# Layer 0 of a four-layer graph network: single-head rows, pair sums in their own buffers, later counts, more kept tiles and a moved quarter of weights

## The chip, the cores and the metric

The kernel runs on one core of a Trainium2 chip. The metric is the device time in microseconds of one execution of the whole program. Three runs of the kernel before took 3268.78, 3267.47 and 3268.74 us; their median is 3268.74.

A core has five engines that run side by side, each in its own order of instructions: TensorE (PE, matrix products; PEld is its loading of weights), VectorE (DVE), ScalarE (ACT), GpSimd (POOL) and SyncE (SP). SP, POOL and ACT also issue transfers between the chip's memory (HBM, "dram" in the code) and the on-chip memory of 128 partitions (SBUF). Matrix products are accumulated in another small memory, PSUM.

## What is computed

Four graph layers follow each other, each with a residual and a layer norm. Only layer 0 is changed. Its input is x (2708 x 512) and a 0/1 matrix adj (2708 x 2708). Both patterns of layer 0 are the same adj.

```python
Xh = X.reshape(n, H, D).transpose(1, 0, 2)          # H = 4 heads, D = 128
Xw = jnp.einsum('hnd,hde->hne', Xh, W)
f1 = jnp.einsum('hnd,hd->hn', Xw, V[:, 0, :, 0])
f2 = jnp.einsum('hnd,hd->hn', Xw, V[:, 1, :, 0])
sig = jax.nn.sigmoid(f1[:, :, None] + f2[:, None, :])
att = softmax(where(adj != 0, adj * sig, -inf))      # 0 outside the mask
Xa = jnp.einsum('hij,hjd->hid', att, Xw)             # first use of att
Xn = batchnorm(Xa)                                   # over the 2708 rows
emb = batchnorm(elu(Xn @ W1.T + b1) + Xn)
Y = jnp.einsum('hij,hjd->hid', att, emb)             # second use of the same att
Y = elu(jnp.einsum('hnd,hed->hne', Y, W))
out = batchnorm(elu(Y @ W2.T + b2) + Y)
```

## The kernel before, in words

**Tiles.** The attention is made transposed: the rows of a tile are 128 values of j, the columns are values of i. There are 22 tiles of j (BLOCKS; the last has only 20 rows) and the 2708 columns are cut in two halves of 1354 (HSPAN). The four heads are taken in two pairs, p = 0 and p = 1. A *block* is one half with one pair; a block has 22 *places*, one tile of j at each, in the order of ORDER (line 154): tiles 0 to 10, the short tile 21, then 11 to 20. A pass over the attention is four blocks: half 0 with pairs 0 and 1, then half 1 with pairs 0 and 1. In this text the first pass (values xw, the output Xa) has blocks 0 to 3, the second (values emb, the output Y) blocks 4 to 7. "5:1" is place 1 of block 5.

**One place** (`form`, line 360, and `attention_pass`, line 336). A row of the mask, a (128 x 1354, 677 KB), is loaded from HBM by SP. The mask is adj itself in blocks 0 and 2, where DVE turns it into 1 and -1e30 (line 389) and POOL writes it back as adj_d; later blocks load adj_d. ACT takes tanh of half of f1 + f2 for each of the two heads (line 400), where f1b holds f1 spread over the partitions, both heads of the pair in one tile, in one of two buffers, and f2 is a bias per partition. DVE multiplies tanh + 1 with the mask row (line 408), a product over both heads at once, 2708 columns. ACT takes exp of it (line 409). The tile t is then multiplied with the values by TensorE (line 478): two heads times three column parts of 452, each matmul in two passes. The six results stay in PSUM over all 22 places. In the second pass DVE also counts, once per tile and half, how many entries of the mask row are zero (`count`, line 342, one instruction on line 350); before, this stands ahead of the tile's tanhs and product, in the block of the pair that isn't read back. There are four t buffers, and four a buffers in the first pass, three in the second.

**Sums of the softmax.** In the first pass a product with ones (line 507, into psm) sums each tile over j. In blocks 0 and 2 every tile is summed. In blocks 1 and 3 the places from 4 to 19 (ALONE, LAST) are summed in pairs: DVE adds the odd tile into the even one (line 498), and TensorE sums the result. The pair's addition and sums are kept back (`waiting`) and put ahead of the matmuls of the next even place, the addition behind that place's product. Since the even tile is overwritten, the addition waits for TensorE to have read it. In the second pass the sums are already known; their inverses are loaded as rb.

**Kept tiles.** Some of the finished t tiles are written to HBM in the first pass by POOL (line 457, 1354 KB each), and read back in the second (line 460) in place of forming them anew. KEPT (line 160) lists their places for each pair: five and five, with place 11 common to both. A common tile is counted in the block of pair 0 from a mask row of its own (line 462).

**Ends of blocks.** A finished block's results leave PSUM before the next block's first matmuls can overwrite them: in the first pass by copies in `keep` (line 590), half of them on ACT, half on DVE; in the second by DVE's multiplication with rb and the batch norm's scale in `decode` (`take`, line 846, six per block).

**Between the passes.** Batch norm 1, the preparation of layer 3's weights, and the MLP with elu and batch norm 2. For layer 3 the product of its two weight matrices is wanted. `merged(c)` (line 696) makes a quarter of it with four matmuls. Two quarters are made here; the other two are made at the end of layer 0, after the last block's dec matmuls (line 985), copied by ACT (line 993) and written by POOL (line 994).

**What sets the order.** Each engine runs its instructions in one fixed order[...]. The program's text gives the work; a planner of the framework sets each engine's order when the kernel is built, by the costs it assumes and by when buffers come free. `tc.issue_after(x)` puts what is inside it behind instruction x. A tile with a tag shares its buffers with all tiles of that tag; a new one waits until the oldest is no longer read.

## Time and profile before

The times come from the three runs, the rest from one execution taken by the profiler.

| what | value |
|---|---|
| median of three runs | 3268.74 us (3267.47 to 3268.78) |
| the profiled execution, its own time | 3272.62 us |
| its span in the trace | 3270.8 us, 30357 instructions |
| PE busy | 3212.9 us, 98% |
| DVE busy | 1944.1 us, 59% |
| ACT busy | 1346.8 us, 41% |
| POOL busy | 132.9 us, 4% |
| transfers | 384.59 MB, mean 118 GB/s |
| DVE product, line 408, 2708 columns | 2976 ns on average, 156 times |
| ACT tanh, line 400, 1354 columns | 1413 ns, 312 times |
| ACT exp, line 409, 2708 columns | 2453 ns, 156 times |
| DVE pair addition, line 498, 2708 columns | 2974 ns |
| DVE count, line 350, 1354 columns | 1562 ns |
| mean granted clock of TensorE | 0.994 |

How to read it: a line of the groups gives source line, engine, operation, what it writes from what, the shape and the number of instructions; behind the first bar the busy time and the mean of one in ns; behind the second the time that the engine idled just before these instructions, and what ended that idling. A line of the chain gives the start and the length in us of a piece of the chain of waits that ended last. A line of the windows gives the busy time of each engine in a stretch, with its number of instructions, then the clock granted to TensorE (1.00 is full speed), the share of the DMA engines and GB/s.

Layer 0 takes about the first 1190 us of the span: block 0 begins at 44.5 us with its first matmul, the middle part lies from 556 to 670 us, and the second pass ends near 1121 us. Layers 1 to 3 follow.

### The profile page before, as it was taken

Reading aid. Unit: us, or ns where it says so; the run is one execution under the profiler, and the core shown is the slowest. Engines: PE = TensorE matmul, PEld = TensorE weight load, DVE = VectorE, ACT = ScalarE, POOL = GpSimd, SP = SyncE. Lnnn points to the kernel's source line nnn. Section 1 sums busy time; section 2 is a strip of 40 time slices with the busy share of each in tenths; the row PEclk is TensorE's granted clock in tenths of the full one; section 3 lists DMA queues with packets and bytes.
Section 4 is the critical chain, followed back from the end, with each engine's and each line's share of the span. In section 5 each row is a group of like instructions: output and inputs, shape, how many; then the busy total and the mean of one; then the engine's idle time right before and its main releaser. Section 6 shows DMA issues by size and latency. Waiting matters only on the chain.

```text
span 3270.8 us, 30357 instructions
## 1 busy us (share of the span) xinstructions
PE 3212.9 (98%) x10906; PEld 1717.4 (53%) x10906; DVE 1944.1 (59%) x3144; ACT 1346.8 (41%) x1512; POOL 132.9 (4%) x215
## 2 busy tenths in 40 slices
PE   8999999999999999999999999999999999999999
PEld 5444444444444446885555555544455555555554
DVE  7878977867687685445136666777353442543433
ACT  6888886567868652001133434443021020110211
POOL 1100100000000000000010000000000000000000
PEclk9999999999999999999999999999999999999999
DMA  7856854245545412550034444553211111111100
GB/s 278 314 187 223 298 200 147 88 152 194 169 163 177 169 53 80 144 133 15 1 118 136 118 124 137 151 160 111 72 47 32 45 35 37 41 34 45 35 24 20
DMA packets 173158, 384.59 MB, mean 118 GB/s; under 512 B 21034, under 2 KB 115190, under 8 KB 168334
## 3 DMA queue, kind: packets, MB, share of 16 engines
q1 hardware_dynamic: 157214, 309.74, 31.1%
q0 software_dynamic: 15792, 72.91, 5.9%
q8 instruction: 86, 1.41, 0.2%
q14 instruction: 66, 0.54, 0.1%
HBM read 308.79 MB, written 73.24 MB: 117 GB/s over the span
## 4 chain that ended last, share of the span: by engine, by line
PE 87%; DVE 6%; ACT 3%; DMA 2%; issue 1%; SPq 0%; DVEq 0%; ACTq 0%
PE po L1377 23%; PE po L478 18%; PE ps_s L1256 17%; PE ps_nb L1109 7%; PE ps_wide L1158 4%; PE psm L507 3%; DVE t L408 2%; PE ps_hid L129 2%; PE ps_sup L1554 2%; PE ps_o L1485 2%; PE ps_dec L880 2%; ACT t L400 2%; ACT t L409 1%; PE ps_mlp L755 1%; DMA a<-adj_d 1%
## 5 line engine op out<-in xcount | busy, mean ns | idle before, releaser
L408 DVE SCALAR_TENSOR_TENSOR t<-t,a 128x2708 f32<-128x2708 f32 (+1 forms) x156 | 462.4, 2976 | 135.2 <-ACT t L400 131.2
L400 ACT ACTIVATE t<-f1b,f2h 128x1354 f32<-128x1354 f32 (+1 forms) x312 | 427.2, 1413 | 63.5 <-PE psm L507 32.1
L409 ACT ACTIVATE t<-t 128x2708 f32<-128x2708 f32 (+1 forms) x156 | 382.2, 2453 | 95.0 <-DVE t L408 94.8
L478 PE MATMUL po<-t,xw 128*128 128x452 f32 (+3 forms) x1056 | 412.9, 553 | 7.7 <-ACT t L409 7.7
L478 PE MATMUL po<-t,emb 128*128 128x452 f32 (+3 forms) x1056 | 403.1, 550 | 12.5 <-ACT t L409 9.2
L1256 PE MATMUL ps_s<-sup,hT 128*128 128x384 f32 (+1 forms) x1176 | 407.4, 490 | 0.0
L1377 PE MATMUL po<-sup,e 128*128 128x512 f32 x882 | 407.1, 595 | 0.2 <-DVE xs L1613 0.2
L1377 PE MATMUL po<-e,xs 128*128 128x384 f32 (+1 forms) x1176 | 406.0, 489 | 0.0
L1688 DVE SCALAR_TENSOR_TENSOR e<-a_cols,ps_s 128x384 f32<-128x384 f32 (+1 forms) x154 | 85.7, 556 | 450.4 <-PE ps_s L1256 427.5
L1256 PEld LDWEIGHTS ps_s<-sup,hT 128*128 128x128 f32 x1176 | 221.8, 190 | 164.2 <-issue 14.2
L478 PEld LDWEIGHTS po<-t,emb 128*128 128x128 f32 (+1 forms) x1056 | 194.9, 192 | 213.6 <-issue 189.2
L1377 PEld LDWEIGHTS po<-e,xs 128*128 128x128 f32 x1176 | 222.2, 190 | 160.2 <-issue 5.8
L478 PEld LDWEIGHTS po<-t,xw 128*128 128x128 f32 (+1 forms) x1056 | 189.1, 191 | 219.9 <-issue 199.9
L1377 PEld LDWEIGHTS po<-sup,e 128*128 128x128 f32 x882 | 160.3, 190 | 159.8 <-issue 136.9
L1256 PE MATMUL ps_s<-hT 128*128 128x384 f32 (+5 forms) x672 | 211.3, 461 | 1.4 <-DVE e L1604 0.8
L1355 ACT ACTIVATE e<-e 128x384 f32<-128x384 f32 (+1 forms) x308 | 151.9, 522 | 116.6 <-DVE e L1354 113.7
L1603 ACT ACTIVATE a_cols<-a_cols,neg_big 128x384 f32<-128x384 f32 (+1 forms) x154 | 94.5, 616 | 232.3 <-DMA a_cols<-in_adjT_dram 187.2
L1109 PE MATMUL ps_nb<-hid_hi,at 128*128 128x512 f32 x484 | 185.5, 390 | 0.4 <-DVE at L1101 0.4
L109 ACT ACTIVATE ln_rstd<-ln_rstd 128x1 f32<-128x1 f32 (+1 forms) x88 | 17.2, 201 | 395.9 <-DVE ln_rstd L108 395.4
L1109 PE MATMUL ps_nb<-hid_lo,at 128*128 128x512 f32 x462 | 180.1, 390 | 0.0
L1354 DVE TENSOR_TENSOR e<-e,nmax 128x384 f32<-128x384 f32 (+1 forms) x308 | 163.8, 555 | 23.3 <-ACT nmax L1347 23.3
L1256 PEld LDWEIGHTS ps_s<-hT 128*128 128x128 f32 x672 | 123.1, 190 | 90.2 <-issue 19.1
(252 smaller groups left out, 3321.0 us busy)
## 6 DMA issues: line engine op xcount, KB each, us to landing
a<-adj_d SPq DMA_DIRECT2D x110, 677.0 KB
a_cols<-in_adjT_dram SPq DMA_DIRECT2D x378, 192.0 KB
a<-in_adjT_dram SPq DMA_DIRECT2D x42, 677.0 KB
adj_d<-a POOLq DMA_DIRECT2D x42, 677.0 KB, 5.8
raw<-in_adjT_dram SPq DMA_DIRECT2D x105, 256.0 KB
kept<-t POOLq DMA_DIRECT2D x16, 1354.0 KB, 6.7
t<-kept SPq DMA_DIRECT2D x16, 1354.0 KB
a_cols<-in_adjT_dram SPq DMA_DIRECT2D x63, 202.0 KB
```

What stands on the lines that cost most here:

```text
L400: nc.scalar.activation(tv[:, k, :], f1b[:n, k, :w], AF.Tanh, bias=f2h[:n, jt, h : h + 1], scale=0.5,)
L408: step = nc.vector.scalar_tensor_tensor(tv, tv, GUARD, ab, ALU.add, ALU.mult)
L409: nc.scalar.activation(tv, tv, AF.Exp, scale=0.5)
L478: nc.tensor.matmul(po[HB * k + q][:, :qw], values[r : r + n, jt, h * P : (h + 1) * P], t[r : r + n, k, q0 : q0 + qw], start=(place == 0), ...
L507: nc.tensor.matmul(sums[k][32 * r : 32 * r + 32, :SW], ones32[:m], whole[:m, k, q0 + qw - SW : q0 + qw], start=first_one, stop=last_one,)
L1109: nc.tensor.matmul(pos[it][:n], at, half[:, jt, :], start=(jt == 0 and k == 0), stop=(jt == NT - 1),)
L1158: nc.tensor.matmul(ps[:, :width], w(c, o), xt(c), start=(c == 0), stop=(c == C - 1),)
L1256: nc.tensor.matmul(ps[:, b * P : w], keys[:, c, j0 : j0 + P], st["q"][:, c, b * P :], start=(c == 0), stop=(c == C - 1),)
L1354: nc.vector.tensor_tensor(e, e, st["nmax"][:, :w], ALU.add)
L1355: nc.scalar.activation(e, e, AF.Exp)
L1377: nc.tensor.matmul(out, lhsT, rhs, start=(k == 0), stop=(k == NT - 1))
L1603: nc.scalar.activation(a, a, AF.Identity, bias=neg_big[: a.shape[0]], scale=1.0e30)
```

## The change

- **Rows of single heads.** f1b is now one tile per head with three buffers (HP + 1) instead of one tile per pair with two. Head 0's row is loaded by SP, as before the pair's was; head 1's is loaded on ACT's queue in the first pass and on POOL's in the second.
- **Pair sums in buffers of their own.** The even and the odd tile of a pair are added head by head into two further buffers (tags z and pair), and no longer in place, except with the short tile. The sums follow the odd tile's matmuls at once; `waiting` is gone.
- **Counts.** A tile's count stands behind its product, and the second pass has four a buffers instead of three.
- **Kept places.** Pair 1 keeps eight places instead of five. Three of them (4, 11, 14) are now common to both pairs.
- **Weights.** Three quarters are merged in the middle and one at the end; its write goes to SP's queue.

```diff
@@ -159,3 +158,3 @@
 
-    KEPT = [(4, 8, 11, 14, 18), (3, 7, 11, 15, 19)]
+    KEPT = [(4, 8, 11, 14, 18), (1, 4, 7, 9, 11, 14, 17, 20)]
     KEPT = [[ORDER[k] for k in places] for places in KEPT]
@@ -167,3 +166,3 @@
 
-    wqT_d = dram.tile([P, C, C // 2 * P], F32, name="wqT_d")
+    wqT_d = dram.tile([P, C, P], F32, name="wqT_d")
     wkT_d = dram.tile([P, C, F], F32, name="wkT_d")
@@ -250,4 +249,6 @@
 
-            stage = att.tile([P, HP, HW], F32, tag="f1b", name="f1_rows", bufs=2)[:, 0, :]
-            f1b = att.tile([P, HP, HW], F32, tag="f1b", name="f1b", bufs=2)
+            stage, *f1b = [
+                att.tile([P, HW], F32, tag="f1b", name=name, bufs=HP + 1)
+                for name in ["f1_rows"] + ["f1b"] * HP
+            ]
 
@@ -270,5 +271,6 @@
             nc.sync.dma_start(f1_d[:, h0 : h0 + w], stage[0 : 32 * H : 32, :w])
-            spread = nc.sync.dma_start(
-                f1b[:, :, :w], f1_d[:HP, h0 : h0 + w].partition_broadcast(P)
-            )
+            for k in range(HP):
+                spread = nc.sync.dma_start(
+                    f1b[k][:, :w], f1_d[k, h0 : h0 + w].partition_broadcast(P)
+                )
             def values_of(jt):
@@ -346,3 +348,3 @@
                 if a is None:
-                    a = att.tile([P, HW], F32, tag="a", name="a", bufs=3)
+                    a = att.tile([P, HW], F32, tag="a", name="a", bufs=4)
                     nc.sync.dma_start(a[:n, :w], adj_d[j0 : j0 + n, h0 : h0 + w])
@@ -367,3 +369,3 @@
                 else:
-                    a = att.tile([P, HW], F32, tag="a", name="a", bufs=4 if first else 3)
+                    a = att.tile([P, HW], F32, tag="a", name="a", bufs=4)
 
@@ -394,4 +396,2 @@
                     nc.gpsimd.dma_start(adj_d[j0 : j0 + m, h0 : h0 + w], a[:m, :w])
-                if not first and p == (jt in KEPT[0]):
-                    count(hf, jt, att, a)
 
@@ -401,3 +401,3 @@
                         tv[:, k, :],
-                        f1b[:n, k, :w],
+                        f1b[k][:n, :w],
                         AF.Tanh,
@@ -409,2 +409,6 @@
                 nc.scalar.activation(tv, tv, AF.Exp, scale=0.5)
+                if not first and p == (jt in KEPT[0]):
+
+                    with tc.issue_after(step.ins):
+                        count(hf, jt, att, a)
                 return step
@@ -423,9 +427,16 @@
                     if f1b is None or not prepare or hf > 0:
-                        f1b = att.tile([P, HP, HW], F32, tag="f1b", name="f1b", bufs=2)
 
-                        with tc.issue_after(loads[-9].ins) if len(loads) > 8 else nullcontext():
-                            nc.sync.dma_start(
-                                f1b[:, :, :w],
-                                f1_d[HP * p : HP * (p + 1), h0 : h0 + w].partition_broadcast(P),
-                            )
+                        early = (
+                            tc.issue_after(loads[-9].ins) if len(loads) > 8 else nullcontext()
+                        )
+
+                        f1b = [
+                            att.tile([P, HW], F32, tag="f1b", name="f1b", bufs=HP + 1)
+                            for k in range(HP)
+                        ]
+                        f1 = f1_d[HP * p : HP * (p + 1), h0 : h0 + w].partition_broadcast(P)
+                        with early:
+                            nc.sync.dma_start(f1b[0][:, :w], f1[:, 0, :])
+                        queue = nc.scalar if first else nc.gpsimd
+                        queue.dma_start(f1b[1][:, :w], f1[:, 1, :])
                     rb = None if first else spread_sums(att, hf, p)
@@ -434,3 +445,3 @@
                         sums = sum_tiles()
-                    before = waiting = None
+                    before = None
                     for place, jt in enumerate(ORDER):
@@ -470,5 +481,2 @@
                             po = [both[q][:, k, :] for k in range(HP) for q in range(HB)]
-                        if waiting is not None:
-                            waiting(step)
-                            waiting = None
                         for k in range(HP):
@@ -488,32 +496,31 @@
 
-
-                        single = prepare or not ALONE <= place < NT - LAST
-                        if not single and place % 2 == 0:
+                        if prepare or not ALONE <= place < NT - LAST:
+                            whole, m = [t[:, k, :] for k in range(HP)], n
+                        elif place % 2 == 0:
                             before = t
                             continue
+                        elif n < P:
+                            whole, m = [before[:, k, :] for k in range(HP)], P
+                            nc.vector.tensor_tensor(
+                                before[:n, :, :w], before[:n, :, :w], tv, ALU.add
+                            )
+                        else:
 
-                        def add_up(whole, m, more, first_one, last_one, behind=None):
-                            if more is not None:
-                                with tc.issue_after(behind.ins):
-                                    nc.vector.tensor_tensor(
-                                        whole[: more.shape[0], :, :w],
-                                        whole[: more.shape[0], :, :w],
-                                        more,
-                                        ALU.add,
-                                    )
-                            for k in range(HP):
-                                for r, (q0, qw) in enumerate(SCH[hf]):
-
-                                    nc.tensor.matmul(
-                                        sums[k][32 * r : 32 * r + 32, :SW],
-                                        ones32[:m],
-                                        whole[:m, k, q0 + qw - SW : q0 + qw],
-                                        start=first_one,
-                                        stop=last_one,
-                                    )
+                            whole, m = [], P
+                            for k, tag in enumerate(("z", "pair")):
+                                both = att.tile([P, HW], F32, tag=tag, name="pair", bufs=1)
+                                nc.vector.tensor_tensor(
+                                    both[:, :w], before[:, k, :w], tv[:, k, :], ALU.add
+                                )
+                                whole.append(both)
+                        for k in range(HP):
+                            for r, (q0, qw) in enumerate(SCH[hf]):
 
-                        if single:
-                            add_up(t, n, None, place == 0, place == NT - 1)
-                        else:
-                            waiting = partial(add_up, before, P, tv, False, False)
+                                nc.tensor.matmul(
+                                    sums[k][32 * r : 32 * r + 32, :SW],
+                                    ones32[:m],
+                                    whole[k][:m, q0 + qw - SW : q0 + qw],
+                                    start=(place == 0),
+                                    stop=(place == NT - 1),
+                                )
                     later += finish(hf, p, po, sums if first else rb) or []
@@ -732,7 +739,8 @@
             nc.gpsimd.dma_start(wkT_d, wkT)
-            nc.gpsimd.dma_start(wqT_d, wqT[:, :, half * P :])
-            merged(1)
+            nc.gpsimd.dma_start(wqT_d, wqT[:, :, (C - 1) * P :])
+            for c in range(1, C - 1):
+                merged(c)
             for o in range(C):
                 nc.gpsimd.dma_start(
-                    mqk_d[o][:, :half, :], mqk[:, :half, o * P : (o + 1) * P]
+                    mqk_d[o][:, : C - 1, :], mqk[:, : C - 1, o * P : (o + 1) * P]
                 )
@@ -974,7 +982,4 @@
                 wk_again = rest[0][:, : C * F].rearrange("p (c o) -> p c o", c=C)
-                wq_again, mqk = [
-                    rest[1][:, k * half * F : (k + 1) * half * F] for k in range(2)
-                ]
-                wq_again = wq_again.rearrange("p (c o) -> p c o", c=C)
-                mqk = mqk.rearrange("p (c o) -> p c o", c=half)
+                wq_again = rest[1][:, : C * P].rearrange("p (c o) -> p c o", c=C)
+                mqk = rest[1][:, C * P : C * P + F]
                 nc.sync.dma_start(wk_again, wkT_d)
@@ -982,17 +987,15 @@
                 with tc.issue_after(last_dec[0].ins):
-                    for c in range(half):
-                        for o in range(C):
-                            nc.tensor.matmul(
-                                po[1 + c],
-                                wq_again[:, o, c * P : (c + 1) * P],
-                                wk_again[:, o, :],
-                                start=(o == 0),
-                                stop=(o == C - 1),
-                            )
-                for c in range(half):
-                    nc.scalar.activation(mqk[:, c, :], po[1 + c], AF.Copy, scale=qscale)
-                    nc.gpsimd.dma_start(
-                        mqk_d[:, :, half + c, :].rearrange("o p i -> p o i"),
-                        mqk[:, c, :].rearrange("p (o i) -> p o i", o=C),
-                    )
+                    for o in range(C):
+                        nc.tensor.matmul(
+                            po[1],
+                            wq_again[:, o, :],
+                            wk_again[:, o, :],
+                            start=(o == 0),
+                            stop=(o == C - 1),
+                        )
+                nc.scalar.activation(mqk, po[1], AF.Copy, scale=qscale)
+                nc.sync.dma_start(
+                    mqk_d[:, :, C - 1, :].rearrange("o p i -> p o i"),
+                    mqk.rearrange("p (o i) -> p o i", o=C),
+                )
 
```

## The prediction

> **What bounds the kernel now.** I read the page from the top, busy shares and groups, and then the chain of waits where it leaves TensorE. The span is 3270.8 us.
>
> ```profile
> PE 3212.9 (98%) x10906; PEld 1717.4 (53%) x10906; DVE 1944.1 (59%) x3144; ACT 1346.8 (41%) x1512; POOL 132.9 (4%) x215
> ...
> L478 PE MATMUL po<-t,emb 128*128 128x452 f32 (+3 forms) x1056 | 403.1, 550 | 12.5 <-ACT t L409 9.2
> ```
>
> TensorE (PE) is busy 98% of the span and the diff removes none of its work in layer 0 (it only moves eight passes of the weight product). So a gain can only come out of TensorE's idle time (the second line's 12.5 us, which counts waits for ScalarE's exp L409, is such time), and out of what its clock loses after it. I took layer 0 stretch by stretch, and listed where two matmuls start further apart than their kind does. The edit reaches blocks 0 to 3 (the first attention pass, 44 to 556 us), the middle (to 670) and blocks 4 to 7 (the second pass, to 1121). With a row of every matmul's start in hand, the gaps sum to about 5.9 us in block 1, 5.3 in block 2, 4.3 in block 3 and 20 in the second pass, clock losses included. The largest, at the switch from block 4 to 5, as the chain of waits tells it:
>
> ```profile
> 764.36 2.98 DVE t L408
> 767.36 3.92 DMA a<-adj_d
> 772.97 2.90 DVE t L408
> 775.90 2.47 ACT t L409
> ...
> 778.40 4.10 PE po L478 x5
> ```
>
> Block 4's last matmul ends at 772.6. VectorE (DVE) is then only finishing a count of zeros (line 350) begun at 771.4 when its mask row had landed, since a buffer for it came free only when the product of 764.36 ended. The next block's first product (L408) stands behind the count, and the four divided results that empty TensorE's accumulators stand behind that product: TensorE idles 6.0 us. The next switch is alike, but there two products stand ahead of the results (L846):
>
> ```profile
> 880.63 5.78 DVE t L408 x2
> 886.41 1.21 DVE ot L846 x2
> ...
> 887.75 4.86 PE po L478 x6
> ```
>
> Third, the pair sums of blocks 1 and 3: each (L498) overwrites a tile that TensorE is reading, so it begins when a matmul ends, and the sum matmuls wait for it. The last three lines are block 2's stall, which ScalarE (ACT) sets:
>
> ```profile
> 230.11 4.76 PE po L478 x12
> 234.96 2.98 DVE t L498
> 237.98 2.16 PE psm L507 x16
> ...
> 365.06 2.74 ACT t L400 x2
> 367.80 2.36 ACT t L409
> 370.20 7.14 PE po L478 x12
> ```
>
> And the windows of 50 us around the three larger stalls, whose PEclk column (the last but two) costs 0.07 x 50 = 3.5 us each:
>
> ```profile
> 350.00:400.00 50.00, 47.73 (x226) 20.48 (x225) 48.45 (x29) 42.74 (x26) 6.44 (x11) 0.93 0.88 305
> 750.00:800.00 50.00, 42.96 (x105) 20.78 (x104) 35.72 (x30) 39.79 (x27) 0.00 (x0) 0.93 0.46 153
> 850.00:900.00 50.00, 46.17 (x114) 22.41 (x113) 36.66 (x29) 40.34 (x25) 0.00 (x0) 0.93 0.51 170
> ```
>
> **The change, part by part.** Its order of instructions can be read from the built program; the durations are from the profiled execution before.
>
> *Counts behind their product, a fourth mask buffer in the second pass.* The count (1.56 us, L350's mean) still runs, but no longer ahead of the product of its own tile, so a late mask row delays no product. DVE waited 30.1 us for mask rows ahead of counts in 13 places; most were hidden. At the 4 to 5 switch the built order is: last product of block 4, its count, product 5:0, the four results. The last product has no reason to end later than 767.36, so product and count are done by 772, 5:0 waits only for its tanhs, and results of 0.6 us spacing start when block 4's matmuls end. The results come in the good order for TensorE (both halves of head 0 first), so I leave 0.3 us. Removed: 6.0 − 0.3 idle and 2.9 of clock, −8.6. Stalls of the same cause within blocks 4, 5 and 7 are 2.6, 0.9 and 0.9: −4.4.
> At the 5 to 6 switch the built order puts products 6:0, count, 6:1 ahead of the results, and the second tanh of 6:0 behind the second head's row load. By hand: the last matmul ends, 6:1 is still running or about to, 2.98 for it and 1.2 for two results less about 1 already elapsed = 3.2, against 3.3 before. So 0 here; −6.4 if 6:1 slips behind the results, +2 if a count also lies in front.
>
> *Eight kept places of heads 2 and 3.* Three more tiles per half: in blocks 5 and 7 this takes 2 x 1.41 + 2.45 = 5.3 us of ACT and 2.98 of DVE per tile away, both there with slack. Its loads are 1354 KB instead of 677, and two more places (4, 14) need a mask row for their count only: 2 x 677 KB per half. DMA is 46 to 51% busy there. In blocks 1 and 3 the Pool queue writes six more tiles, 6.7 us from issue to landing, holding one of four t buffers that long; a place takes TensorE 4.6 us, so a buffer is held about as long as matmul and sums hold it today. Zero in the sum, −1 to +3 in the range: if that cover goes, a tanh is late by up to 2 us.
>
> *Pair sums in own buffers.* One add of 2.98 becomes two of about 1.5 (by width: 1354 of 2708; L390 has 1.57 for that width). They no longer wait for TensorE, and the sums follow the odd tile's matmuls. By hand in block 1: the built DVE order is product 12, 13, pair, 14, so exp 14 ends about 9.0 us after exp 13, where TensorE needs it after about 6.0 plus 0.7 of lead: a stall of 2.3 once, at place 14. The short tile of 20 rows is still added in place and waits as before, 1.4. Before: 5.9. Block 1: −2.2 (−5 to +1.5); block 3, with less to remove: −0.6 (−4 to +3). In block 2 the built order of ACT has exp 12 after one tanh of 14, not after two as in the chain (2.74 for both): 1.4 of the 2.34 stall goes, and perhaps the lost clock: −2.5 (0 to −5.3).
>
> [...] The two-head window at 350 us shows a stall of 2.34 followed by half speed, 0.93 over 50 us. [...] by the row it may cost 2.3 + 3.0, which would turn block 1 from −2.2 to +0.8. Stalls of 1.6 and 1.4 elsewhere were followed by full speed. I take 2.3 and put 5.3 in the range: [...] the row says it can happen.
>
> *Rows of single heads.* The load of 1354 KB at a block's start becomes two of 677. A mask row of that size took 3.67 to 3.92 from issue to use. Head 0 is loaded early by SP, past nothing new. Head 1 goes on ACT's queue (first pass; behind tanhs of place 21) or Pool's (second pass), since its buffer is that of the block before, free after its last tanh. In the second pass about 5 us lie between that tanh and the tanh that needs it: 0.53 to issue and about 4 to land, so it is just in time. ACT loses three issues of about 0.4 in the first pass, 0 on the path. At the start of the kernel the first product stood behind a mask of the next tile (z L389 at 35.06, product at 35.92); now it follows its two tanhs, about 34.4: −1.3 (0 to −1.8).
>
> *Weights.* Three quarters instead of two in the middle: 8 passes at 0.43 us (L985's spacing) = 3.4 on a TensorE busy 68.4 of 70 us there. One place of it is already idle (1.15 us), so +2.5 (0 to +4). At the end 8 passes fewer (3.4), one copy of 0.60 instead of two, but the third normalization's chain of small DVE and ACT steps sets that end: −0.4 (0 to −1).
>
> **Sum.** −1.3 − 2.2 − 2.5 − 0.6 + 2.5 − 8.6 − 4.4 + 0 − 0.4 = −17.5; with a few tenths of new gaps, −17. The profiled execution took 3272.6 (span 3270.8 and 1.8 around it), the three runs 3267.5 to 3268.8, median 3268.7. The profile is 0.1% above; its differences I carry over to the median: 3268.7 − 17 = **3252**. Layers 1 to 3 have the same order of instructions and only shift.
>
> **Rivals.**
> - *Also the 5 to 6 switch and block 1 come out clean*: 6:1 falls behind the results (−6.4) and exp 14 is in time (−2.3 and −1.5 in block 3): about 3241. For it: ACT and DVE have more slack in block 5 with eight kept tiles. Against: the built order has 6:1 ahead of the results.
> - *The gain goes off the path*: the results at 4 to 5 stand behind a late 5:0 (its tanh waits for the second head's row), so 4 to 5 keeps 5 of its 8.9; pair sums ahead of the next product stall three places instead of one (+5), and the middle pays 3.4: −17 + 5 + 5 + 1 = −6: 3263, within or near no change.
> - *Slower: the second head's row is late at every switch.* Its issue waits for the last tanh, and it is a broadcast to 128 partitions; the kernel's first one, of two heads, was used 8.3 us after issue. The slack is 5 us plus 1.8 of lead, less 0.5 to issue. Below 6 us of landing it costs nothing; at 11 it stalls TensorE by about 4.8 and loses about 3 of clock, at three switches of the second pass: +23.4, less 17: 3275. That is the point from which it decides (a landing of 11 or more). Against: half the bytes of the 8.3, so an estimate of 4.2 by bytes.
>
> **How the numbers follow.** The likeliest case 0.55, clean 0.18, off the path 0.18, late rows 0.09. Range 3239 to 3266: the clean case with a little more, to the off-path case with the middle's and block 1's upper bounds (+1.5, +1.5). The likeliest alone: 3246 to 3259. A change under 0.2%, 6.5 us, can't be told from none here. Faster: 0.55 + 0.18 + a third of the 0.18 off the path = 0.79; same: its other two thirds, 0.12; slower: the late rows, 0.09.
>
> **What would show it.** In the profile after: no gap above 1 us at the 4 to 5 switch, PEclk 1.00 over 750 to 800; DVE's wait for mask rows ahead of counts well below 30 us; the pair add at 1.5 us waiting for no matmul; one stall near place 14 of block 1; ACT's tanh waiting for f1b at no switch by more than 1.5 us; the middle about 2.5 longer. Wrong it would be if f1b appears as releaser of tanhs with several us, if PEclk falls in blocks 1 or 3, or if results L846 still start behind a product at 4 to 5.

## The result and the profile after

The changed kernel takes 3257.57 us in the median of six runs (3254.74 to 3259.96); the kernel before, run beside it, 3268.76 us. The ratio is 0.9965, with a 95% interval of 0.9952 to 0.9978. So the change gains 11.2 us where 17 were forecast. The direction and the range (3239 to 3266) held; the gain was put half as large again as it is.

The profiled execution of the changed kernel took 3256.93 us, with a span of 3255.2. That is 15.7 us under the profiled execution before, more than the medians differ by, because the profile before (3272.62) is itself 3.9 above its runs. The table compares the two profiles stage by stage, by the starts of TensorE's matmuls; it must be read with those 4.5 us in mind (15.7 less 11.2). About 2.2 of them lie in layers 1 to 3, whose instructions are the same and in the same order.

| stage (us) | before | after | moved | forecast |
|---|---|---|---|---|
| start to the first attention matmul | 44.44 | 43.73 | −0.7 | −1.3 |
| block 0 | 129.57 | 130.02 | +0.4 | 0 |
| block 1 | 124.55 | 123.58 | −1.0 | −2.2 |
| block 2 | 134.25 | 132.30 | −1.9 | −2.5 |
| block 3 | 123.91 | 124.08 | +0.2 | −0.6 |
| middle, first weight transpose to first matmul of block 4 | 113.46 | 117.88 | +4.4 | +2.5 |
| block 4 with the switch to 5 | 108.22 | 101.13 | −7.1 | |
| block 5 with the switch to 6 | 109.36 | 106.73 | −2.6 | |
| block 6 | 129.58 | 128.86 | −0.7 | |
| block 7 | 103.00 | 101.68 | −1.3 | |
| blocks 4 to 7 together | 450.16 | 438.40 | −11.8 | −13.0 |
| end of layer 0 to layer 1's neighbour sum | 156.85 | 153.78 | −3.1 | −0.4 |
| the rest | 1987.02 | 1984.86 | −2.2 | 0 |

The page of the changed kernel, busy time of TensorE and the group of the second pass's matmuls:

```profile
PE 3211.0 (99%) x10906; PEld 1719.3 (53%) x10906; DVE 1926.2 (59%) x3152; ACT 1317.1 (40%) x1494; POOL 138.1 (4%) x223
...
L486 PE MATMUL po<-t,emb 128*128 128x452 f32 (+3 forms) x1056 | 398.2, 546 | 5.6 <-DVE ot L854 4.5
```

The matmuls are the same, 1056 of them; the idle time in front of them fell from 12.5 us to 5.6, and what ends most of it is no longer an exp but the taking of results (L854). DVE at the 4 to 5 switch, in order of time (start, length, instruction, and in brackets what it idled for):

```profile
765.15 1.56 DVE L352 TENSOR_SCALAR_CACHE_REDUCE z<-a 128x1354 uint8<-128x1354 f32 x1
766.63 0.08 DVE L352 DVE_READ_ACCUMULATOR z<-a 128x1 f32 x1
766.63 2.97 DVE L408 SCALAR_TENSOR_TENSOR t<-t,a 128x2708 f32<-128x2708 f32 x1
771.31 1.88 DVE L854 SCALAR_TENSOR_TENSOR ot<-po,bn_scale,rb 128x452 f32<-128x452 f32 x3 [1.70 <-PE po L486]
```

Count, product of 5:0, and then DVE is free and waits 1.70 us for TensorE, not TensorE for DVE: the 6 us stall is gone. At the 5 to 6 switch the chain of waits reads:

```profile
873.96 2.98 DVE t L408
876.94 1.29 DVE ot L854 x3
878.23 0.41 issue
878.65 0.69 DVE ot L854
879.33 0.14 issue
879.47 2.60 PE po L486 x3
```

Here the product of 6:1 still stands ahead of the four results, and TensorE idles 4.7 us (3.3 before). The windows of 50 us confirm both, by their PEclk column (1.00 in the second line, 0.93 in the third); the first line is block 2's, 0.97 where the kernel before had 0.93:

```profile
350.00:400.00 50.00, 49.04 (x243) 20.82 (x243) 48.28 (x28) 44.23 (x27) 6.35 (x12) 0.97 0.81 287
750.00:800.00 50.00, 50.00 (x132) 24.81 (x132) 39.56 (x34) 42.16 (x28) 0.57 (x1) 1.00 0.74 260
850.00:900.00 50.00, 45.49 (x114) 22.38 (x113) 36.28 (x36) 37.03 (x25) 0.54 (x1) 0.93 0.55 196
```

Block 1, DVE around place 14:

```profile
237.42 2.96 DVE L408 SCALAR_TENSOR_TENSOR t<-t,a 128x2708 f32<-128x2708 f32 x1
242.90 3.05 DVE L512 TENSOR_TENSOR pair<-t 128x1354 f32<-128x1354 f32 x2 [2.53 <-ACT t L409]
245.87 8.75 DVE L408 SCALAR_TENSOR_TENSOR t<-t,a 128x2708 f32<-128x2708 f32 x3
```

Product 13, the pair's two additions, product 14. The product waits 3.0 us behind the additions, its exp runs from 249.4, and place 14 begins at 251.84 after a TensorE stall of 2.44 us. The forecast had 2.3 there.

### The profile page after: what moved, and what is told of

Read it like the earlier page. It is cut to its first block, busy times and chain, and to the rows that moved or that the text cites. A ratio compares the mean times of both kernels' runs of the same rounds, so it can differ in the third digit from the quotient of the medians.

```text
span 3255.2 us, 30397 instructions
## 1 busy us (share of the span) xinstructions
PE 3211.0 (99%) x10906; PEld 1719.3 (53%) x10906; DVE 1926.2 (59%) x3152; ACT 1317.1 (40%) x1494; POOL 138.1 (4%) x223
## 3 DMA queue, kind: packets, MB, share of 16 engines
q8 instruction: 86, 1.41, 0.2%
## 4 chain that ended last, share of the span: by engine, by line
PE 88%; issue 6%; DVE 2%; ACT 2%; DMA 1%; SPq 0%; POOL 0%; DVEq 0%; ACTq 0%; POOLq 0%
PE po L1380 23%; PE po L486 18%; PE ps_s L1259 18%; PE ps_nb L1112 7%; PE ps_wide L1161 4%; PE psm L519 3%; PE ps_hid L128 2%; PE ps_sup L1557 2%; PE ps_o L1488 2%; PE ps_mlp L763 2%; PE ps_dec L888 2%; PE ps_s L1251 1%; ACT t L400 1%; ACT t L409 1%; PE tp L1151 1%
## 5 line engine op out<-in xcount | busy, mean ns | idle before, releaser
L408 DVE SCALAR_TENSOR_TENSOR t<-t,a 128x2708 f32<-128x2708 f32 (+1 forms) x150 | 444.6, 2975 | 155.0 <-ACT t L400 151.2
L400 ACT ACTIVATE t<-f1b,f2h 128x1354 f32<-128x1354 f32 (+1 forms) x300 | 412.0, 1414 | 67.9 <-PE po L486 31.3
L409 ACT ACTIVATE t<-t 128x2708 f32<-128x2708 f32 (+1 forms) x150 | 367.3, 2453 | 88.7 <-DVE t L408 88.4
L1259 PEld LDWEIGHTS ps_s<-sup,hT 128*128 128x128 f32 x1176 | 221.8, 190 | 164.2 <-issue 14.2
```

The costliest lines, as they stand in the source:

```text
L400: nc.scalar.activation(tv[:, k, :], f1b[k][:n, :w], AF.Tanh, bias=f2h[:n, jt, h : h + 1], scale=0.5,)
L408: step = nc.vector.scalar_tensor_tensor(tv, tv, GUARD, ab, ALU.add, ALU.mult)
L409: nc.scalar.activation(tv, tv, AF.Exp, scale=0.5)
L1259: nc.tensor.matmul(ps[:, b * P : w], keys[:, c, j0 : j0 + P], st["q"][:, c, b * P :], start=(c == 0), stop=(c == C - 1),)
```

## The experiments

Each kernel is the changed one with an edit, unless it says otherwise. The kernel before ran beside them, with medians of 3269.6, 3268.7 and 3269.6 us in the three groups, so kernels are compared by their gain over the one before beside them:

| kernel | median us | gain us | ratio, 95% interval |
|---|---|---|---|
| the change | 3257.57 | 11.2 | 0.9965 (0.9952 to 0.9978) |
| count ahead of its product | 3268.47 | 1.1 | 0.9997 (0.9989 to 1.0005) |
| three mask buffers | 3255.03 | 14.6 | 0.9955 (0.9943 to 0.9968) |
| five kept places as before | 3262.80 | 6.8 | 0.9980 (0.9974 to 0.9987) |
| two quarters in the middle | 3254.80 | 14.8 | 0.9956 (0.9944 to 0.9968) |
| pair sums in place | 3259.00 | 9.7 | 0.9969 (0.9956 to 0.9981) |
| also rows of both heads, three mask buffers | 3256.03 | 12.7 | 0.9958 (0.9943 to 0.9973) |
| results ahead of place 1 | 3252.80 | 15.9 | 0.9950 (0.9936 to 0.9965) |
| pair sums one place later | 3256.32 | 12.4 | 0.9960 (0.9945 to 0.9975) |
| five kept places with place 1 | 3258.36 | 11.2 | 0.9959 (0.9945 to 0.9972) |
| eight without place 1 | 3259.59 | 10.0 | 0.9968 (0.9957 to 0.9980) |
| two parts on the kernel before | 3255.43 | 14.2 | 0.9956 (0.9943 to 0.9968) |
| the same, results ahead of place 1 | 3255.61 | 14.0 | 0.9958 (0.9946 to 0.9971) |

The intervals are some 4 us to each side for most: differences of 3 us between two of these kernels are not told apart by their times, and those of 4 to 5 only barely; they need the stage in the profile to stand. Each kernel has one profile, and its stages are those of that one execution.

### The count ahead of its product again

```diff
+                if not first and p == (jt in KEPT[0]):
+                    count(hf, jt, att, a)
                 for k in range(HP):
...
-                if not first and p == (jt in KEPT[0]):
-                    with tc.issue_after(step.ins):
-                        count(hf, jt, att, a)
```

> The changed kernel with one part undone: the count of zeros stands ahead of the tile's tanhs and product again; the fourth mask buffer stays. My theory (the order made the gain at the 4 to 5 switch and inside blocks 4, 5 and 7): block 4 takes 106 to 108 us again instead of 101.1, with a gap above 4 us at the 4 to 5 switch and a granted clock of 0.93 around it; the median is 3265 (8 above the changed kernel's 3257.6). Rival (the fourth buffer made it, since the mask row then lands before it is needed): block 4 stays within 1.5 us of 101.1 and the median within 2 us of 3257.6.

Measured: a gain of 1.1 us, not to be told from none. This one edit takes back nearly the whole gain, although everything else of the change stays. It does so elsewhere than I expected. Block 4 takes 106.6 us, but there is no gap at the 4 to 5 switch; the time goes into stalls of 2.0, 3.4 and 1.4 us inside block 4. Block 5 takes 111.9, with a gap of 7.0 us at the 5 to 6 switch. Its chain there:

```profile
869.11 4.81 DMA f1b<-f_d
...
878.41 3.87 DMA a<-adj_d
...
882.39 0.10 DVE z L352
882.49 1.39 issue
883.88 0.08 DVE z L352
883.96 2.90 DVE t L410
...
886.89 2.47 ACT t L411
```

A mask row of 3.87 us, the count that waited for it, the product behind the count, the exp: the mechanism of the forecast, one switch further on. Two things go beyond it. This row is loaded on line 350, so the count is that of a tile kept by both pairs, which the edit does not touch itself and which the order now puts ahead of the last product before the results. And the chain starts with the second head's row of f1, 4.81 us on POOL's queue: in this kernel the late row of the forecast's last rival has a part in the gap. DVE's wait for mask rows ahead of counts is 22.2 us in the second pass of this kernel; the changed kernel has no such wait at all.

### Three mask buffers

```diff
-                    a = att.tile([P, HW], F32, tag="a", name="a", bufs=4)
+                    a = att.tile([P, HW], F32, tag="a", name="a", bufs=4 if first else 3)
```

and likewise in `count`.

> The changed kernel with three mask buffers in the second pass as before; the count stays behind its product. Theory (order): block 4 within 1.5 us of 101.1 and the median within 2 us of 3257.6. Rival (buffer): block 4 at 106 to 108 and the median near 3265. If both this and the kernel with the count ahead stay fast, either part alone is enough; if both are slow, both are needed.

Measured: a gain of 14.6 us, block 4 at 100.2. The fourth buffer brings nothing that a run shows; the order of the count does.

### Five kept places of pair 1 as before

```diff
-    KEPT = [(4, 8, 11, 14, 18), (1, 4, 7, 9, 11, 14, 17, 20)]
+    KEPT = [(4, 8, 11, 14, 18), (3, 7, 11, 15, 19)]
```

> The changed kernel with pair 1 keeping five places (3, 7, 11, 15, 19) as before. Prediction's step (zero in the sum): median within 2 us of 3257.6, blocks 5 and 7 within 1 us of 106.7 and 101.7. Rival A (the three tiles spared are what removed the small stalls in blocks 5 and 7, 0.9 + 0.9, and ACT's room at the switches): 2 to 4 us slower, all of it in blocks 5 and 7. Rival B (the six more writes cost in blocks 1 and 3): blocks 1 and 3 each 1 to 2 us shorter than 123.6 and 124.1, median about 3255.

Measured: a gain of 6.8 us, in 21 runs that spread from 3257.5 to 3268.8. So without the new kept places 4.4 us of the gain are gone (only four of the 21 runs lie below the slowest of the changed kernel, 3259.96), and none of the three expectations had the place: the loss is at the 4 to 5 switch. Its profiled execution (3268.80, the slowest of its runs) has the gap back there, 6.5 us, and the clock is lost behind it (0.83 over 770 to 790 us). That is more than the median lost, so the gap cannot be as long in all of its runs. DVE at that switch:

```profile
767.80 2.98 DVE L408 SCALAR_TENSOR_TENSOR t<-t,a 128x2708 f32<-128x2708 f32 x1
774.62 2.98 DVE L408 SCALAR_TENSOR_TENSOR t<-t,a 128x2708 f32<-128x2708 f32 x1 [3.84 <-ACT t L400]
777.52 1.87 DVE L854 SCALAR_TENSOR_TENSOR ot<-po,bn_scale,rb 128x452 f32<-128x452 f32 x3
```

There are two products ahead of the results, 5:0 and 5:1, where the changed kernel has one. Place 1 of block 5 is kept in the new list and formed in the old one, so the planner has a product (and two tanhs) to put in front of the results. That led to the next two kernels.

### Place 1, or the number of kept tiles

Five with place 1, and eight without it:

```diff
-    KEPT = [(4, 8, 11, 14, 18), (1, 4, 7, 9, 11, 14, 17, 20)]
+    KEPT = [(4, 8, 11, 14, 18), (1, 7, 11, 15, 19)]
```

```diff
-    KEPT = [(4, 8, 11, 14, 18), (1, 4, 7, 9, 11, 14, 17, 20)]
+    KEPT = [(4, 8, 11, 14, 18), (3, 4, 7, 9, 11, 14, 17, 20)]
```

> The changed kernel with pair 1 keeping five places as many as before, but place 1 among them (1, 7, 11, 15, 19). Theory (with place 1 kept, no product 5:1 is formed ahead of the results at the 4 to 5 switch; the number of kept tiles matters little): no gap above 1 us there, block 4 at 101 to 101.5, median 3257 to 3259, and a narrow spread of runs. Rival (eight tiles give ACT and DVE the room): as with places 3, 7, 11, 15, 19, so block 4 near 108.7 in a profile with the gap, median 3262.8.

> The changed kernel with pair 1 keeping eight places, but place 3 instead of place 1 (3, 4, 7, 9, 11, 14, 17, 20). Theory (place 1): the gap of about 6.5 us at the 4 to 5 switch is back in some or all executions, median 3261 to 3264. Rival (the number): no gap, block 4 within 1 us of 101.1, median within 2 us of 3257.6.

Measured: gains of 11.2 us with place 1 and five tiles, 10.0 with eight and without it. In the profile of the first, DVE does as in the changed kernel: one product, then a wait for TensorE, and no gap of 1 us at the switch.

```profile
766.87 2.97 DVE L408 SCALAR_TENSOR_TENSOR t<-t,a 128x2708 f32<-128x2708 f32 x1
771.36 3.66 DVE L854 SCALAR_TENSOR_TENSOR ot<-po,bn_scale,rb 128x452 f32<-128x452 f32 x6 [1.51 <-PE po L486]
```

In the second the product of 5:1 is back ahead of the results, but ACT has tanh ready early and the product starts at 766.67, not 774.62:

```profile
763.44 2.98 DVE L408 SCALAR_TENSOR_TENSOR t<-t,a 128x2708 f32<-128x2708 f32 x1
766.67 2.98 DVE L408 SCALAR_TENSOR_TENSOR t<-t,a 128x2708 f32<-128x2708 f32 x1 [0.25 <-ACT t L400]
769.57 3.66 DVE L854 SCALAR_TENSOR_TENSOR ot<-po,bn_scale,rb 128x452 f32<-128x452 f32 x6
```

That leaves a gap of 2.2 us and a window of 12 us at a granted clock of 0.86. So by the medians place 1 alone brings back the whole 4.4 us, and the number alone 3.2, a difference of the size that the times don't tell: each looks like a way to clear the same switch, and they don't add. My theory (the place, and the number matters little) is shown in its first half only; that place 1 does better than the number rests on the 2.2 us gap in the profile, since the times of the two overlap.

### Two quarters in the middle, two at the end

The weights' lines as they were before.

> The changed kernel with two quarters of the weight product in the middle and two at the end as before. From the two profiles: the middle comes back by 4.4 us (117.9 to 113.5), the end of layer 0 (last attention matmul to the first matmul of layer 1's neighbour sum) goes up by 3.1 us (153.8 to 156.9): median 1.3 us faster, 3256. The prediction's own terms (+2.5 and -0.4) would make it 2.1 faster, with the end of layer 0 longer by only 0.4.

Measured: a gain of 14.8 us, 3.6 more than the whole change has. But the stages don't bear that out: the end of layer 0 goes to 157.3 us (+3.5) and the middle to 115.4 (−2.5), a loss of 1.0 together. A second pair of kernels further down, with and without the third quarter in the middle, has 3.3 there against 3.0 at the end, and medians 0.6 apart. So the quarter moves about 3 us from the end to the middle, and what the whole gains or loses by it is too small to tell. The end shows what the forecast left out. In the kernel before, the first transposed output of the norm waited for ACT's second copy of the product, and TensorE was busy with the product until 1.75 us before it; in the changed kernel it starts as soon as DVE's part is ready:

```profile
1186.09 1.10 PE L1049 MATMUL tp_out<-ident,ot 128*128 128x128 f32 x8 [1.75 <-ACT wq_again L993]
```

```profile
1173.97 0.44 PE L1052 MATMUL tp_out<-ident,ot 128*128 128x128 f32 x2 [3.39 <-DVE ot L1046]
```

Before, the product and its copy bound this point, not the norm's chain; with one quarter less the chain does, and TensorE idles 3.39 us for it.

### Pair sums in place; and rows of both heads

```diff
-                            for k, tag in enumerate(("z", "pair")):
-                                both = att.tile([P, HW], F32, tag=tag, name="pair", bufs=1)
...
+                            waiting = partial(add_up, before, P, tv, False, False)
```

> The changed kernel with the pair sums of blocks 1 and 3 in place again, kept back to the next even place as before. Prediction's step (own buffers are worth 2.2 in block 1 and 0.6 in block 3): those blocks at 125.8 and 124.7, the median at 3260. Rival (own buffers only trade several small stalls for one of 2.4 us at place 14): blocks 1 and 3 within 1 us of the 124.6 and 123.9 of the kernel before, the median within 2 us of 3257.6.

> The changed kernel with the rows of f1 of both heads in one tile and one load again; the room for that is had by three mask buffers in the second pass and pair sums in place. What is left of the change: counts behind their product, eight kept places, three quarters in the middle. If single-head rows are worth what the prediction says (1.3 at the start, nothing after): first matmul of block 0 at 44.4 instead of 43.7, and the rest as with pair sums in place, median 3259 to 3261. Rival (their late second head costs at the 5 to 6 switch, where the tanh waited 1.6 us for it): block 5 at 104 to 105 instead of 106.7 and the median at 3256.

Measured: with pairs in place a gain of 9.7 us, and blocks 1, 2 and 3 at 124.7, 136.7 and 121.4. Against the changed kernel that is +1.1, +4.4 and −2.7. So own buffers bring 1.1 in block 1, take 2.7 in block 3, and what they bring most lies in block 2, which has no pairs. With pairs in place that block keeps the stall of 2.3 us that the kernel before had and has another of 1.9 about 35 us earlier; why block 2 (which starts on what block 1 left behind) differs so was not followed up. In the times they bring 1.5 us, less than runs can tell.

With rows of both heads in one tile on top, and three mask buffers, the gain is 12.7: 3.0 more, which only the stages can bear out. Rows of single heads gain at the start (the first matmul at 42.2 to 43.8 us in the ten kernels that have them, against 44.4 to 45.1 in the four without) and lose in two other places. One is the wait at the 5 to 6 switch: block 5 at 105.5. The other one was in nobody's expectation, the middle: 115.2 us against 117.6. The three mask buffers are not the reason: alone they leave the two at 106.8 and 117.8. ACT of the changed kernel there:

```profile
566.73 0.20 ACT L108 ACTIVATE bn_scale<-bn_scale 128x4 f32<-128x4 f32 x1 [3.68 <-DVE bn_scale L107]
569.98 1.28 ACT L400 ACT_TABLE_LOAD   x1 [3.05 <-DMA f1b<-f_d]
571.28 1.42 ACT L400 ACTIVATE t<-f1b,f2h 128x1354 f32<-128x1354 f32 x1
572.61 0.58 ACT L713 ACTIVATE emb<-ps_m 128x512 f32<-128x512 f32 x1
```

and of the kernel with rows of both heads:

```profile
570.63 0.21 ACT L109 ACTIVATE bn_scale<-bn_scale 128x4 f32<-128x4 f32 x1 [3.68 <-DVE bn_scale L108]
573.25 0.60 ACT L707 ACTIVATE emb<-ps_m 128x512 f32<-128x512 f32 x1 [2.42 <-PE ps_m L700]
575.71 1.28 ACT L398 ACT_TABLE_LOAD   x1 [1.87 <-DMA f1b<-f_d]
577.01 1.43 ACT L398 ACTIVATE t<-f1b,f2h 128x1354 f32<-128x1354 f32 x1
```

A single head's row lands earlier (the table load that waits for it starts 3.25 us after the norm's scale, 569.98 − 566.73, against 5.08 for the row of both heads, 575.71 − 570.63), so the planner puts its tanh, with 1.28 us of loading the function table, ahead of the copy of the first merged quarter. The copy starts 5.9 us after the norm's scale (572.61 − 566.73) instead of 2.6 (573.25 − 570.63), the merge behind it waits for its accumulator (TensorE idles 0.46 us for the copy at 573.24), and TensorE's clock is 0.97 over the middle's first 50 us instead of 1.00.

### Results ahead of the next block's place 1

```diff
-                    for k in range(HP):
-                        for q in range(HB):
-                            take(k, q)
+                    for q in range(HB):
+                        for k in range(HP):
+                            taken_b[q, k] = take(k, q)
...
-                                for ins in taken.values() if place == 2 else ():
+                                for ins in taken.values() if place == (2 if first else 1) else ():
```

> The changed kernel with two things added in the second pass: the results of a finished block are taken in the order both heads of a column part, then the next part, and place 1 of the next block is formed behind them. If the 4.7 us gap at the 5 to 6 switch is the product of 6:1 standing ahead of the results: gap under 1 us there, no loss of clock, block 5 at 99.5 to 100.5 instead of 106.7, median 3251. Rival (the switch waits for the tanh and exp of 6:0, which come late with the second head's row): the gap stays above 3 us and the median within 2 us of 3257.6.

Measured: 3252.80 us (3252.63 to 3253.47), a gain of 15.9 and the fastest of all. Block 5 falls to 102.2, and the gap at the switch is gone, so the product of 6:1 was its cause. But part of it comes back one place later, 3.2 us: the exp of 6:1 now stands behind ACT's first elu of block 5 as the chain shows, and block 6 takes 2.5 us more. In the profiles the second pass gains 2.0 us by the edit; another 1.4 of its lead over the changed kernel lies ahead of the first attention matmul, where the edit does not reach.

```profile
878.45 0.77 PE ps_y L881 x2
879.22 0.02 issue
879.25 0.55 ACT elu_m L535
879.79 2.36 ACT t L409
882.15 0.04 issue
882.19 2.14 PE po L486 x3
```

### Pair sums one place later

The additions, in their own buffers, go behind the product of the next even place, the sums behind that place's matmuls.

> The changed kernel with the additions of a pair, still in buffers of their own, put behind the product of the next even place, and its sums behind that place's matmuls. If the stall at place 14 (2.4 us, then 1.5 us of clock) comes from the pair's two additions ahead of product 14: blocks 1 and 3 at 120 to 121 each instead of 123.6 and 124.1, median 3251. Rival (tiles are then held longer, so a later tanh waits for its buffer): the stall moves to another place and both blocks stay within 1 us of 123.6.

Measured: a gain of 12.4 us, not to be told from the changed kernel. The stall at place 14 goes from 2.4 to 0.9, so the additions were its cause, but stalls of 1.1 at the sums, 1.6 near the end of block 1 and 4.0 in the first places of block 2 take its place; block 1 stays at 124.0, block 3 falls to 121.5, block 2 rises to 136.5. The rival was right for block 1 and for the time; block 3, which it had within 1 us of 123.6, did fall.

### Two parts alone

The kernel before with the count behind its product and the eight kept places, and nothing else; then the same with the results ahead of place 1.

> The kernel before with two parts of the change only: counts behind their product, and pair 1's eight places. Rows of both heads in one tile, pair sums in place, three mask buffers and two quarters in the middle stay as they were. If these two parts carry the whole gain and the third quarter costs 2.8: 3256.0 less 2.8 = 3253, 4 below the whole change. Rival (the parts left out add up with others to something): above 3257.

> The same two parts on the kernel before, and in the second pass the results of a block in the order of column parts, with place 1 of the next block formed behind them. From the 4.8 us that this brought on the changed kernel: 3253 less 4.8 = 3248. Rival (the gap only moves to place 1 of block 6, 3.2 us there, as it partly did on the changed kernel): 3251 to 3253.

Measured: gains of 14.2 and 14.0 us. Two of the five parts carry the whole gain; the three others together bring nothing that these runs show. Which of the two would do alone on the kernel before was not tried. On this base the results ahead of place 1 gain nothing in the median: the profile shows block 5 down to 102.2 and block 6 up to 131.2 as on the changed kernel, 0.2 us net, and a longer block 2. On the changed kernel it was 2.0 net; the rest of the 4.8 stays open. A kernel with that edit and two quarters on the changed kernel was not tried.

## Why the prediction was right or wrong

- **Counts behind their product, −13 in the second pass**: measured −11.8, and the mechanism shown by undoing it. What failed is the attribution. I read the order at the 4 to 5 switch, one product and then the results, from the built program and put it down to the counts. That order needs place 1 of block 5 to be kept. With the old places 4.4 us of the gain are not had.
- **Eight kept places, "zero in the sum"**: wrong, 4.4 us. I priced the tiles by the room that they give ACT and DVE and not by the product that disappears from the order at a switch. That the writes cost something was right in kind: in the first pass ACT waited 8.5 us for written tiles (1.5 before), hidden for the most part.
- **The 5 to 6 switch, 0**: 4.7 us of idle time for 3.3, in the given bounds of −6.4 to +2.
- **Pair sums, −2.2 and −0.6**: −1.0 and +0.2. The stall at place 14 was put at 2.3 and came at 2.44, in block 1 and also in block 3, where I had not counted it. And the clock term was mis-sized: after it the clock fell (0.87 over 249 to 262 us). Block 2, −2.5: −1.9, and as forecast: its stall fell from 2.34 us to 1.03, and its time at half clock from 6.8 us to 3.4.

The windows behind that stall, in the changed kernel and in the kernel with three mask buffers, whose stall at this place was 0.8:

```profile
249.00:262.00 13.00, 10.62 (x31) 4.88 (x24) 11.34 (x5) 12.02 (x8) 0.55 (x1) 0.87 0.77 267
```

```profile
251.00:263.00 12.00, 11.27 (x52) 5.15 (x48) 10.34 (x5) 10.45 (x6) 0.55 (x1) 1.00 0.81 285
```

The first costs 1.7 us of clock, the second nothing at this place. But the second kernel had lost the same 1.7 us already 14 us earlier, behind the stall of 1.4 us at the short tile. TensorE came to place 14 later and stalled there for 1.6 us less: the place begins 78.1 us into the block in both. So the same loss is hidden when it falls ahead of this wait and paid when it falls behind it. The kernel before had one behind its short tile too. The windows there, first the kernel with three mask buffers, then the kernel before:

```profile
237.00:249.00 12.00, 10.59 (x39) 4.83 (x37) 9.47 (x5) 8.99 (x6) 0.00 (x0) 0.86 0.19 59
```

```profile
236.00:248.00 12.00, 10.59 (x41) 4.56 (x36) 9.96 (x4) 11.58 (x7) 0.00 (x0) 0.86 0.55 180
```

So the prediction's "Stalls of 1.6 and 1.4 elsewhere were followed by full speed" does not hold for this stall, and the 5.9 us of block 1 that it worked from held a clock loss of 1.7. Block 1 has one such loss before and after; block 3 had none and has one. In the three kernels whose block 1 is the changed kernel's and whose loss fell early (count first, three mask buffers, two quarters) that block took 122.0 to 122.3 us, 2.2 to 2.6 below the kernel before, which is what the forecast had; in the changed kernel's own execution it fell late. That nothing is lost behind a stall of 2.3 us was my assumption, which no trace had shown; the row of before, with 0.93 over 50 us behind its stall of 2.34, spoke against it. The row was right: all eleven stalls of 2.44 us at place 14, in seven kernels, were followed by a clock of 0.84 to 0.87 over 11 to 13 us. The forecast had no clock loss left in blocks 1 and 3; this is 1.7 us in each, more than the 1.2 and 0.8 by which those blocks fell short of the forecast.

- **Weights, +2.5 and −0.4**: +4.4 and −3.1. The end was mis-read: the step "the third normalization's chain of small DVE and ACT steps sets that end" failed, since product and copy did. In the middle the third quarter costs 3.3 (115.2 with it and 111.9 without, both with rows of both heads), counts and kept places together give 1.5 back (113.5 before, 111.9), and the missing term is the 2.4 of the next point.
- **Rows of single heads, −1.3 at the start**: about right, 44.4 or more against 42.2 to 43.8. The second head's row was in time: its loads landed 3.9 to 7.0 us after issue, 4.1 in the median, and its tanh waited once, 1.6 us. The slower rival needed 11. With the counts back in front the row did stand in the chain of the 5 to 6 switch. What I didn't see is that a row that lands *earlier* moves a tanh ahead of a copy in the middle: 2.4 us.
- **The sum.** Layer 0 moved −13.4 in the profiles where the terms made −17.5: the second pass fell 1.2 short, the first 3.0, the middle 1.9 and the start 0.6, and the end gave 2.7 more. The other 2 us between −13.4 and the measured −11.2 probably belong to the execution that I took my rows from, which was 3.9 us slower than the median of its own kernel; where in it they lie was not traced. So part of the closeness of the total is luck: the end's 2.7 more than forecast hid a part of what the first pass and the middle fell short.
- **The rivals.** "Off the path" happened in part: the middle paid in full and the pair sums stalled. "Clean" did not happen at 5 to 6, and the kernel that made it happen showed the gap coming back at place 1.

## What to carry to other kernels

When a built order is what a forecast rests on, ask which edit made that order before crediting one; a list of cached tiles can matter through *which* instruction vanishes ahead of a hand-over, and not only through the load that it takes away. An instruction that may wait for a late transfer belongs behind the ones that others wait for; without that single move hardly any of the gain was left here (1.1 of 11.2 us), and one more buffer for the transfer, which that kernel had, did not replace it. And a transfer that lands earlier is not free: it can let its consumer in ahead of something more urgent on the same engine, as in the middle here, for 2.4 us.

## What the runs showed of the hardware

TensorE's clock fell after the stalls of 2.44 us at place 14, to 0.84 to 0.87 over 11 to 13 us, which is 1.7 us of lost time, eleven times of eleven. It is not the stall's length alone: in block 2 of the changed kernel a stall of 1.03 us was followed by a clock of 0.83 over 10 us (366 to 376), and a stall of 1.63 us in the kernel with later pair sums by a clock of 1.00 over 12 (276 to 288). Nor is it certain after a longer one: with the count first, block 4's stall from 749.8 to 753.0 us was followed by full clock (1.00 over 748 to 762), and so was one of 2.6 us in block 1 of the kernel with pair sums in place (1.00 over 275 to 288).

In layer 0 of the profiles before and after, each loss is a stretch of 3.41 or 6.83 us at a clock of 0.50. From block 1 on the changed kernel has them at 252.87, 368.92, 508.87 and 577.14 us (3.41 each), 877.51 and 1174.47 (6.83 each); the kernel before at 238.39 (3.41), 368.09, 777.69, 886.92 and 1187.29 (6.83 each). In each trace these starts lie whole multiples of 3.413 us apart, the length of one short stretch: 34, 75, 95, 183 and 270 of them behind the first after, 38, 158, 190 and 278 before. First the changed kernel behind place 14, then the kernel with the count first behind the stall that cost nothing:

```profile
252.88:256.29 3.41, 3.41 (x5) 1.36 (x5) 3.41 (x3) 3.41 (x3) 0.00 (x0) 0.50 0.94 276
```

```profile
748.00:762.00 14.00, 10.76 (x29) 5.19 (x28) 8.35 (x3) 11.08 (x7) 0.00 (x0) 1.00 0.32 99
```

The idle time ahead of a stretch does not tell by itself whether one comes: in the kernel before, TensorE's idle 1.41 us from 236.57 was followed by one (0.86 over 236 to 248), and the same 1.41 us from 495.19 (1.00 over 492 to 505) and 1.42 from 529.82 (1.00 over 527 to 540) were not. What decides it was not shown: no run shifted a stall on purpose to test this.

Also, one program's executions spread by 0.8 to 11 us here (results ahead of place 1, 3252.6 to 3253.5; five kept places, 3257.5 to 3268.8), so that one profile's stages can differ from the medians by as much as a whole part of the change is worth.
